# Norms and reciprocals spread over rows through DRAM instead of TensorE transposes, an earlier second load, and a changed order of shares and closings in a two-layer convolution-attention kernel

## The chip, the cores and the metric

The kernel runs on one core of one Trainium2 chip. The metric is the device time of one execution in microseconds (us). Three timed executions of the kernel before gave 1650.42, 1654.32 and 1650.83 us; the median is 1650.83 us. The operands of all products are stored as float32.

The engines are named as in the profile: PE is TensorE's matmul, PEld its weight load, DVE is VectorE, ACT is ScalarE, POOL is GpSimd, and SP is SyncE, which here only issues DMAs. An engine's name with a q behind it (SPq) is that engine's sequencer.

## The reference

The input x has 4 images of 32 channels by 128 x 128 pixels. Layer 0 folds each 2 x 2 block of pixels into channels: an image is then 128 channels of 64 x 64 = 4096 positions. The attention is between positions: the energy of two of them is the product of their 128 channels divided by the two positions' norms. Layer 1 takes the result as 4096 tokens of 128 values per image: a linear attention (all its products are sums over tokens, without a softmax), then a router and the two best of eight experts.

```python
xs = fold(x)                                   # 2x2 pixels into channels
q = xs.reshape(B, C * R * R, hw)
energy = einsum('bci,bcj->bij', q, q)          # 4096 x 4096 for each image
d = sqrt(diagonal(energy))
energy = energy / (d[:, :, None] * d[:, None, :])
attn = softmax(energy, axis=-1)
out = einsum('bcj,bij->bci', q, attn)
x = unfold(gamma * out + xs)
t = tokens(x)                                  # 4096 tokens of 128 values per image
t = t + linear_attention(layer_norm(t), Wk, Wq, Wv)
t = t + top2_experts(layer_norm(t), router_w, router_b, expert_w, expert_b)
```

The energy matrix of an image is 4096 x 4096 and symmetric. The kernel divides every position's channels by the position's norm before the product (`qn`). Two vectors per image have to be turned from "one value per partition" (a position on each partition) into "one value per column" (positions along the free dimension, the same on every partition): the reciprocal norms, which scale q, and the reciprocals of the softmax's sums times gamma, which scale the output.

## The kernel before, in words

**The attention of an image (`attend`).** The 4096 positions are cut into 8 chunks of 512. For each row i of chunks and each column jc up to i, four steps j each compute 128 x 512 energies (`pe`, line 609), which ACT turns into exponentials with their sums (`pr`, line 612); two steps later the values are multiplied in (`po`, line 497). Because the matrix is symmetric only the lower half is computed. The mirrored half comes from the same exponentials. DVE turns them in blocks of 32 x 32 (`F`, line 421), SP stores them in DRAM (`blocks<-F`, line 530) and reads them back with the blocks exchanged (`F<-blocks`, line 545), and PE then multiplies them in as a "transposed share" (`transposed_share`, `pg`, line 433), four matmul steps per tile, while ACT sums the same tile (`junk`, line 438) and DVE adds the result into `o` (line 442).

**The order is written out by hand.** All instructions of PE, DVE, ACT and SP stand in the order in which the Python code issues them; POOL's own order is left to the scheduler but for pinned instructions. `attend` is a generator that yields twice per step. A virtual `clock` advances by the work issued: 8 for a full energy step and 4 for a share step. A share may start when the clock has moved on by `LAG` = 57 since its tile's reload was issued; `step_share` runs one share step if the oldest is due. `after(n, f)` runs f n steps later. Around this run side streams: entries of `timed` (steps of a generator spread between two percentages of an image's clock; every count is two steps of the generator), and `steady` closings, stepped about once per attention step.

**Preparation of a pair of chunks (`prep`, `prep_first`).** Four DMAs load the pair (`xa`), DVE turns it (`turn_quarters`), squares and sums it (`squares`), POOL takes the power of -1/2 (line 164). To spread the norms along rows, DVE copies them 64 wide (`wide`, line 388), PE transposes that in four pieces (`pnorm`, line 399), and DVE multiplies the pair's channel rows by the result (`scale`, line 372) to give `qn`, the operand of both sides of `pe`. The very first pair (`prep_first`) is instead scaled before it is transposed (`ptn`, line 344). There are 16 pairs of chunks: one goes through `prep_first`, 15 through `pnorm`.

**The closing of an image (`layer1`).** From 84% of an image's clock on, its closing runs beside the next image's attention. `close_rows(kc)` for kc = 0 to 3 waits until the chunks 2kc and 2kc+1 are complete, takes the reciprocals of the sums (`den`, `rd`), copies them 64 wide (`rdx`, line 749), has PE transpose them (`pbd`, line 771), multiplies `o` by them into `df` (line 758), adds that to the tokens `T`, and takes the layer norm's statistics (`bs_a`, `close_stats`: six small DVE instructions, then POOL's power). ACT then normalises four rows of tokens at a time (`normalise`, line 696), and PE adds up their products (`pgram`). `attention_rows(u)` for u = 0 to 3 applies the linear attention (`pat`), takes statistics again, computes the router's logits and normalises; after u = 1 and u = 3 `sorted_experts` sorts tokens by expert, scatters and gathers them with POOL's indirect DMAs (`place` holds their places), and stores the image. The last image has nothing beside it: what is left of its closing (`last_parts`) is the end of the kernel.

**SP's queue.** SP issues nearly all DMAs, in order. DMAs share eight completion semaphores in rotation, and a DMA is issued only when the one eight places before it on its semaphore has landed.

Of the kernel before, what the change touches and what calls it, by code (L numbers as in the profile page):

```python
# [22 lines left out]
def kernel(  # L23
# [278 lines left out]
    def load_quarters(b, kc, queues=(nc.sync, nc.sync)):  # L302

        xa = xin.tile([P, 2, 2, 2, HW2, 2], F32, tag="xx", name=f"xa_{b}_{kc}")
        halves = x[b].rearrange("c (s g) w -> c s (g w)", s=2)
        for a in (0, 2, 1, 3):
            first_row = 16 * kc + 4 * a
            queues[a // 2].dma_start(
                xa[ts(a, S)].rearrange("p s k r w e -> p s (k r w e)"),
                halves[:, :, first_row * W : (first_row + 4) * W],  # L310
            )
        return xa

    def turn_quarters(s, xa, qT):
        for k in range(2):
            nc.vector.transpose(
                qT[:, s, 2 * k : 2 * k + 2, :].rearrange("p h (e r c) -> p r (h e) c", e=2, r=2),
                xa[:, s, k].rearrange("p r (h t) e -> p (r h) e t", h=2),
            )

    def prep_first(st):

        b, kc = 0, 0
        st["T"] = big1.tile([P, KT, D], F32, tag="T", name="T_0")
        xa = load_quarters(b, kc, (nc.sync, nc.scalar))
        qT = chunks_of(b, kc, st)
        yield
        ss = stat.tile([P, 2 * NJ], F32, tag="ss", name=f"ss_{b}_{kc}")
        rn = stat.tile([P, 2 * NJ, 1], F32, tag="rn", name=f"rn_{b}_{kc}")
        for s in range(2):  # L330
            turn_quarters(s, xa, qT)
            squares(b, kc, s, qT, ss)
            pow_neg_half(rn[:, ts(s, NJ), 0], ss[:, ts(s, NJ)])
        keep_running(40, ps_g, "pg")
        scaled = []
        for s in range(2):
            qs = work.tile([P, NJ, P], F32, tag="qs", name=f"qs_{b}_{kc}_{s}", bufs=2)
            nc.vector.tensor_tensor(qs, qT[:, s], rn[:, ts(s, NJ)].to_broadcast([P, NJ, P]), ALU.mult)
            scaled.append(qs)
        for s, qs in enumerate(scaled):  # L340
            qn = channels(b, kc, s, st)
            pt, done = hold(f"ptn_{b}_{kc}_{s}", lambda p, qn=qn: nc.scalar.activation(qn, p, AF.Copy))  # L342
            for j in range(NJ):
                nc.tensor.transpose(pt[:, ts(j, P)], qs[:, j, :], ident)
            done()
            yield

    def prep(b, kc, st):
# [3 lines left out]
        ahead = 2 if b == 0 and kc == 1 else 5  # L352
        xa = load_quarters(b, kc)
# [3 lines left out]
        for _ in range(ahead):  # L357
            yield
        qT = chunks_of(b, kc, st)
        for s in range(2):  # L360
            turn_quarters(s, xa, qT)
            yield
# [15 lines left out]
        rn = stat.tile([P, 2 * NJ, 1], F32, tag="rn", name=f"rn_{b}_{kc}")  # L378
        for s in range(2):
            squares(b, kc, s, qT, ss)  # L380
            if s == 1:
                pow_neg_half(rn[:, :, 0], ss)
            yield
        for _ in range(ahead - 2):
            yield
        wide = work.tile([P, NJ, 2, 64], F32, tag="qs", name=f"wide_{b}_{kc}", bufs=2)
# [3 lines left out]
        if b:  # L390
            yield
# [21 lines left out]
    def after(ticks, f):  # L413
        queued.append((tick[0] + ticks, f))
# [59 lines left out]
    def attend(b, st):  # L474
# [11 lines left out]
        for i in range(NCH):  # L486
# [94 lines left out]
            for jc in order:  # L581
# [21 lines left out]
                for j in range(NJ):  # L603
# [10 lines left out]
                    own.append(pr)  # L614
                    if ending and jc == order[-1] and j == NJ - 1:
                        st["exps"] = True
                    after(2, partial(values, pr[:, c0:], t, c0, CH))
                    if jc < i and not both:
                        after(1, partial(nc.vector.transpose, Fb[:, :, :, j, :], pr))
                        if j == NJ - 1:  # L620
                            after(2, partial(move, F, i, jc))
                    elif jc == i and not ending:
                        if j < NJ - 1:
                            after(1, partial(turn_blocks, F, pr, j))
                        if j == NJ - 2:
                            after(2, partial(move_diagonal, F, i))
                    elif jc == i and j in (1, 2):

                        after(1 if j == 2 and order[-1] == i else 2, partial(below, own, (2, 1) if j == 1 else (3,)))
                    turn_tick()  # L630
                    clock[0] += 2 * (CH - c0) // P
                    step_share()
# [21 lines left out]
    def layer1(b, st):  # L654
# [9 lines left out]
        place = stat.tile([P, 2, KT], U32, tag="place", name=f"place_{b}")  # L664
# [63 lines left out]
        def close_rows(kc):  # L728
# [10 lines left out]
            while "exps" not in st if last_rows else missing():  # L739
                yield from idle(1)  # L740
            while b > 0 and kc == 0 and not states[b - 1].get("sorted"):
                yield from idle(1)
# [3 lines left out]
            wide = work.tile([P, NJ, 2, 64], F32, tag="grp", name=f"rdx_{b}_{kc}", bufs=2)  # L746
            for s in range(2):
                one = rd[:, ts(s, NJ)][:, :, None]
                nc.vector.tensor_scalar(wide[:, :, s], one.to_broadcast([P, NJ, 64]), gam, None, ALU.mult)
            df = work.tile([P, 8, HW2, 2], F32, tag="df", name=f"df_{b}_{kc}", bufs=1)  # L750

            def divide(pb):
                for s in range(2):
                    own = slice(s * 64, s * 64 + 64)
                    o = st["o"][2 * kc + s]
                    for r2 in range(2):
# [4 lines left out]
                            pb[own].rearrange("p (j a t) -> p a j t", a=4, t=S),  # L761
# [3 lines left out]
            yield  # L765
            if not last_rows:
                yield
                yield
            pb, done = hold(f"pbd_{b}_{kc}", divide)
            for j in range(NJ):  # L770
                nc.tensor.transpose(pb[:, ts(j, P)], wide[:, j].rearrange("p s c -> p (s c)"), ident)
            yield
            while missing():
                yield from idle(1)
            done()
# [4 lines left out]
            nc.vector.tensor_tensor(tk, tk, df.rearrange("p k w r -> p k (w r)"), ALU.add)  # L780
            bs, stats = batch_stats("a", 8 * kc, 8)
            for j in range(8):
                stats[j]()
                if j == 3:
                    yield
                    yield
            close_stats("a", 8 * kc, 8, bs)
# [155 lines left out]
        def attention_rows(u):  # L943
# [17 lines left out]
            for j in range(8):  # L961
                stats[j]()
                if j == 3:
                    yield
                    yield
            logits = router_rows(nc.vector, 8 * u, 8, la)
            close_stats("f", 8 * u, 8, bs)
            next(logits)
            yield
# [450 lines left out]
    next(first)  # L1420
    load_weights()
    next(first)
    next(second)
    load_tokens(states[0]["T"][:, 0:8, :], 0, 0, 8)

    ordered = ExitStack()
    ordered.enter_context(tc.manual_schedule(engines=ENGINES))
    timed = [(first, 0, 1, 2), (second, 0.5, 5.5, 10)]
    for b in range(B):
# [36 lines left out]
        if b + 1 < B:  # L1466
            timed.append((prep(b + 1, 2, nxt), 0.5, 16, 17))
            timed.append((prep(b + 1, 3, nxt), 38, 62, 17))
# [43 lines left out]
```

## Time and profile before

The profiled execution took 1650.83 us, of which the span from the first to the last instruction is 1649.0 us.

| | before |
|---|---|
| median of 3 runs | 1650.83 us |
| profiled execution, its span | 1650.83 us, 1649.0 us |
| PE busy | 1609.9 us, 98% of the span |
| DVE, ACT, POOL busy | 931.5, 898.5, 593.8 us |
| DMA moved | 345.37 MB, 212 GB/s over the span |
| granted TensorE clock, mean | 0.996 |

A group row of the profile names the line, the engine and the operation, what is written and read, the count, then the busy time, the mean length of one instruction in ns, and the idle time of the engine just before it with what ended that idle time. Matmuls overlap, so a row's mean length is more than the spacing of two of them. In a row of waits, the total is followed by the number of waits and the longest one. In the timeline, the first two numbers are start and length in us.

### The profile page before, as it was taken

The numbers are of one execution on the slowest core, as the hardware profiler recorded it, in microseconds if no ns is written. First come the engines' busy times: TensorE is split into PE (matmuls) and PEld (weight loads), VectorE is DVE, ScalarE is ACT, GpSimd is POOL, SyncE is SP. The second block draws the span as 40 slices with busy tenths as digits, with TensorE's granted clock in tenths as the row PEclk, the third lists the DMA queues.
The fourth block names the chain that finished last, engine by engine and source line by source line (L and its number), as shares of the span: only waits on it lengthen the run. The fifth ranks groups of instructions, "written<-read, shape, count | busy, mean of one in ns | idle before, by whom it ended". The sixth has DMA issues, their size and how long they took to land.

```text
span 1649.0 us, 21309 instructions
## 1 busy us (share of the span) xinstructions
PE 1609.9 (98%) x5192; PEld 846.5 (51%) x5192; DVE 931.5 (56%) x2383; ACT 898.5 (54%) x2839; POOL 593.8 (36%) x565
## 2 busy tenths in 40 slices
PE   8999999999999999999999999999999999999987
PEld 4444544455554455555554455555554455555633
DVE  4543353567586443549478443448658634345786
ACT  3555445466475555547556455556656555545386
POOL 1000000001015441446555543256555652437166
PEclk9999999999999999999999999999999999999999
DMA  4655656676759777997899777798699877886001
GB/s 143 205 179 178 197 187 213 222 231 204 168 196 283 239 222 220 266 257 200 211 221 287 253 236 241 222 268 230 196 209 279 275 248 236 248 251 192 14 14 39
DMA packets 304297, 345.37 MB, mean 209 GB/s; under 512 B 82096, under 2 KB 230704, under 8 KB 289840
## 3 DMA queue, kind: packets, MB, share of 16 engines
q1 hardware_dynamic: 269712, 304.50, 59.9%
q0 software_dynamic: 26624, 25.58, 7.6%
q10 hardware_dynamic: 7840, 13.93, 2.9%
q8 instruction: 44, 0.72, 0.2%
q14 instruction: 77, 0.63, 0.1%
HBM read 167.08 MB, written 182.09 MB: 212 GB/s over the span
## 4 chain that ended last, share of the span: by engine, by line
PE 81%; DVE 7%; DMA 5%; ACT 3%; SPq 2%; issue 1%; POOL 1%; ACTq 0%; DVEq 0%; POOLq 0%
PE po L497 24%; PE pe L609 23%; PE pg L433 20%; PE pys L1130 3%; PE py L1304 3%; PE pg L453 2%; PE pys L1137 2%; PE pgram L725 2%; DMA F<-blocks 1%; DVE F L421 1%; DMA blocks<-rows 1%; SPq L938 1%; ACT pr L612 1%; ACT xn L696 1%; DMA blocks<-F 1%
## 5 line engine op out<-in xcount | busy, mean ns | idle before, releaser
L612 ACT ACTIVATE pr<-pe 128x512 f32<-128x512 f32 (+1 forms) x576 | 322.4, 560 | 547.5 <-PE pe L609 507.0
L497 PE MATMUL po<-pr,qT 128*128 128x512 f32 (+3 forms) x1152 | 549.4, 559 | 4.2 <-ACT o L502 3.9
L609 PE MATMUL pe<-qn,qn 128*128 128x512 f32 x896 | 458.8, 594 | 4.6 <-ACT pr L612 4.6
L433 PE MATMUL pg<-F,qT 128*128 128x512 f32 x880 | 449.8, 593 | 4.7 <-DMA F<-blocks 4.7
L421 DVE STREAM_TRANSPOSE F<-pr 128x512 f32<-128x512 f32 x440 | 305.4, 700 | 134.5 <-ACT pr L612 124.7
L497 PEld LDWEIGHTS po<-pr,qT 128*128 128x128 f32 x1152 | 215.2, 190 | 250.2 <-issue 217.9
L1178 POOL DMA_INDIRECT acc<-ys,place x128 | 202.1, 1579 | 209.1 <-ACT pr L612 134.8
L438 ACT ACTIVATE junk<-F 128x512 bf16<-128x512 f32 x440 | 273.0, 620 | 4.9 <-DMA F<-blocks 4.9
L433 PEld LDWEIGHTS pg<-F,qT 128*128 128x128 f32 x880 | 166.8, 190 | 199.4 <-issue 182.3
L1066 POOL DMA_INDIRECT xs<-xn,place x192 | 186.0, 969 | 184.1 <-ACT pr L612 118.9
L609 PEld LDWEIGHTS pe<-qn,qn 128*128 128x128 f32 x896 | 155.6, 191 | 119.1 <-issue 106.7
L442 DVE TENSOR_TENSOR o<-o,pg 128x512 f32<-128x512 f32 x110 | 75.1, 683 | 205.4 <-PE pg L433 205.2
L1112 DVE TENSOR_TENSOR results<-pys,xn 128x256 f32<-128x256 f32 x120 | 49.9, 416 | 187.2 <-ACT xn L1106 168.5
L164 POOL TENSOR_TENSOR rn<-ss,neg_half 128x8 f32<-128x8 f32 (+1 forms) x17 | 27.2, 1602 | 320.0 <-DVE ss L296 319.9
L612 ACT ACTIVATION_READ_ACCUMULATOR pr<-pe 128x1 f32 x576 | 111.9, 194 | 0.0
L1106 ACT ACTIVATE xn<-pys 128x256 f32<-128x256 f32 x120 | 45.2, 377 | 111.4 <-PE pys L1137 111.4
L1130 PEld LDWEIGHTS pys<-ew_sb,xn 128*128 128x128 f32 x468 | 70.5, 191 | 52.2 <-issue 49.7
L609 PE MATMUL pe<-qn 128*128 128x512 f32 (+3 forms) x256 | 91.4, 440 | 0.7 <-ACT qn L342 0.7
L1178 POOL DMA_INDIRECT yb<-ys,place x64 | 60.8, 950 | 81.1 <-DMA F<-blocks 31.1
L438 ACT ACTIVATION_READ_ACCUMULATOR junk<-F 128x1 f32 x440 | 84.5, 192 | 0.0
L1130 PE MATMUL pys<-ew_sb,xn 128*128 x468 | 71.6, 275 | 0.0
L1304 PE MATMUL py<-ew_sb,xn 128*128 128x512 f32 x128 | 61.5, 622 | 5.1 <-ACT tmp L1260 3.9
(217 smaller groups left out, 1463.2 us busy)
## 6 DMA issues: line engine op xcount, KB each, us to landing
blocks<-F SPq DMA_DIRECT2D x110, 1024.0 KB
F<-blocks SPq DMA_DIRECT2D x220, 192.0 KB
F<-blocks SPq DMA_DIRECT2D x220, 128.0 KB
xn<-xs SPq DMA_DIRECT2D x114, 132.0 KB
ys<-results SPq DMA_DIRECT2D x114, 128.0 KB
F<-blocks SPq DMA_DIRECT2D x220, 64.0 KB
below<-F SPq DMA_DIRECT2D x31, 384.0 KB
T<-in_x_dram SPq DMA_DIRECT2D x64, 128.0 KB
```

Source lines behind the costliest of these rows:

```text
L421: f()
L433: nc.tensor.matmul(pg.rearrange("p (a f) -> p a f", a=4), st["qT"][i][:, ib, :], G[:, :, ib], start=(ib == 0), stop=(ib == NJ - 1),)
L438: nc.scalar.activation(junk, G[:, :, ib], AF.Copy, accum_out=st["sums"][:, NJ * i + ib, jc : jc + 1])
L442: nc.vector.tensor_tensor(st["o"][jc], st["o"][jc], pg, ALU.add)
L497: nc.tensor.matmul(row["po"][:, lo:hi], qT[blk // NJ][:, blk % NJ, :], w, start=start, stop=(row["left"] == 0))
L609: nc.tensor.matmul(pe[:, c0:], qn[jc][:, ts(j, P)], qn[i][:, c0:], start=True, stop=True)
L612: nc.scalar.activation(pr[:, c0:], pe[:, c0:], AF.Exp, accum_out=sums[:, t, i : i + 1]).ins
L1066: inst = nc.gpsimd.indirect_dma_start(xs[h], offset(place[:, i, k : k + 1]), xn[:, k, :], None)
L1112: nc.vector.tensor_tensor(result[:, :n], p[:, 2 * P : 2 * P + n * D].rearrange("p (j c) -> p j c", c=D), bufs[g % 6][:, :n, D : D + 1].to_ ...
L1130: nc.tensor.matmul(p[:, 2 * P + j * D : 2 * P + j * D + D], bufs[6 + g % 2][:, j, :D], weights[:, bass.ds(begins[2 * (g % 2) + j], D)], st ...
L1178: inst = nc.gpsimd.indirect_dma_start(to, None, ys, offset(place[:, i, k : k + 1]), compute_op=op)
L1304: nc.tensor.matmul(bank, xn[:, k, :D], ew_sb[:, 4 * h : 4 * h + 4, :], start=True, stop=True)
```

## The change

The change has seven parts.

1. A new generator `spread_over_rows` writes a 128 x 32 tile of norms with DVE's block transpose, stores it in DRAM (16 KB), and reads it back with two DMAs, each of which puts the same 4 x 128 values on 64 partitions (128 KB each). It takes the place of the 64-wide copy, the four PE transposes and their PSUM bank in 14 of the 15 calls of `prep` (all but the second pair of image 0), and in `close_rows` for kc < 3 (12 of the 16 calls). The norms sit in three constant tiles, set to 1.0 by POOL at the start.
2. `close_rows` for kc < 3 computes its reciprocals as soon as its sums are complete (`seen`), and not only when `o` is; new sets `divided` and `added` keep the order among the closings of an image.
3. The second pair of image 0 is loaded into a `work` buffer right behind the first, ahead of the weights' and the tokens' loads; its turns stand between the DVE instructions of `prep_first`; its later steps run from 1.3% of the clock instead of 0.5%.
4. `prep_first` turns and squares the second half while POOL takes the first half's power, and the 40 warming transposes are issued first.
5. In a row's first tile at step 2, a share step is taken before the values' matmul instead of after it, if one is due at that earlier clock.
6. `close_rows` has one more yield ahead of `close_stats` (except in the last image's late rows), and `attention_rows` three more around `close_stats` and the first half of the logits.
7. `place` has one buffer instead of two; the next image's fourth pair is prepared at 36 to 54% instead of 38 to 62%.

```diff
-    def load_quarters(b, kc, queues=(nc.sync, nc.sync)):
-        xa = xin.tile([P, 2, 2, 2, HW2, 2], F32, tag="xx", name=f"xa_{b}_{kc}")
+    def load_quarters(b, kc, queues=(nc.sync, nc.sync), place=(xin, "xx")):
+        xa = place[0].tile([P, 2, 2, 2, HW2, 2], F32, tag=place[1], name=f"xa_{b}_{kc}")
...
+    norms = [const.tile([P, S], F32, tag=f"norm{n}", name=f"norm_{n}") for n in range(3)]
+    for norm in norms:
+        nc.gpsimd.memset(norm, 1.0)
...
-        for s in range(2):
-            turn_quarters(s, xa, qT)
-            squares(b, kc, s, qT, ss)
-            pow_neg_half(rn[:, ts(s, NJ), 0], ss[:, ts(s, NJ)])
-        keep_running(40, ps_g, "pg")
...
+        keep_running(40, ps_g, "pg")
+        summed(0, rows_squared(0))
+        sq = rows_squared(1)
+        st["turns"].pop(0)()
+        scale_rows(0)
+        summed(1, sq)
+        st["turns"].pop(0)()
+        st["turns"].pop(0)()
+        scale_rows(1)
+        st["turns"].pop(0)()
...
+    def spread_over_rows(norm, nm, tag, spread, gap):
+        turned = stat.tile([P, S], F32, tag="turned", name=f"turned_{nm}")
+        nc.vector.transpose(turned, norm)
+        yield
+        kept = dram.tile([P, S], F32, tag="norms", name=f"norms_{nm}", bufs=3)
+        nc.sync.dma_start(kept, turned)
+        for _ in range(gap):
+            yield
+        wide = work.tile([P, CH], F32, tag=tag, name=f"spread_{nm}", bufs=2)
+        for s in range(2):
+            nc.sync.dma_start(
+                wide[ts(s, 64)].rearrange("p (a f) -> p a f", a=4),
+                kept.rearrange("(a q) t -> a (q t)", q=S)[:, ts(s, P)].partition_broadcast(64),
+            )
+        spread.append(wide)
+        for _ in range(gap):
+            yield
...
+        if not on_chip:
+            yield from idle(1)
+            yield
+            spread = []
+            yield from spread_over_rows(norm, f"{b}_{kc}", "qs", spread, 5)
+            for s in range(2):
+                scale(s, spread[0], lambda ap: ap.rearrange("p (a j t) -> p a j t", a=4, t=S))
+            yield
+            return
...
+                    starts = jc == order[0] and j == 2
+                    if starts:
+                        step_share()
                     turn_tick()
                     clock[0] += 2 * (CH - c0) // P
-                    step_share()
+                    if not starts:
+                        step_share()
...
-        place = stat.tile([P, 2, KT], U32, tag="place", name=f"place_{b}")
+        place = stat.tile([P, 2, KT], U32, tag="place", name=f"place_{b}", bufs=1)
...
+            far = kc < 3
+            while not summed() if far else "exps" not in st if last_rows else missing():
                 yield from idle(1)
             den, rd = (stat.tile([P, 2 * NJ], F32, tag=nm, name=f"{nm}_{b}_{kc}") for nm in ("den", "rd"))
             nc.vector.tensor_reduce(den, st["sums"][:, ts(kc, 2 * NJ), :], AX.X, ALU.add)
             nc.vector.reciprocal(rd, den)
+            if far:
+                norm = norms[2]
+                nc.vector.tensor_scalar(norm[:, : 2 * NJ], rd, gam, None, ALU.mult)
+                spread = []
+                yield from spread_over_rows(norm, f"den_{b}_{kc}", "grp", spread, 5)
...
             while missing():
                 yield from idle(1)
-            done()
+            if far:
+                divide(spread[0])
+            else:
+                done()
+            st["divided"].add(kc)
...
+            if not late_rows:
+                yield
             close_stats("a", 8 * kc, 8, bs)
...
+            yield
             logits = router_rows(nc.vector, 8 * u, 8, la)
             close_stats("f", 8 * u, 8, bs)
+            yield
             next(logits)
             yield
+            yield
             nc.sync.dma_start(t2[:, ts(u, 8)], T[:, ts(u, 8), :])
...
-    next(first)
-    load_weights()
-    next(first)
-    next(second)
+    next(first)
+    next(second)
+    load_weights()
+    ordered.enter_context(tc.manual_schedule(engines=ENGINES))
+    next(second)
+    next(first)
     load_tokens(states[0]["T"][:, 0:8, :], 0, 0, 8)
...
-    timed = [(first, 0, 1, 2), (second, 0.5, 5.5, 10)]
+    timed = [(first, 0, 1, 2), (second, 1.3, 5.5, 8)]
...
-            timed.append((prep(b + 1, 3, nxt), 38, 62, 17))
+            timed.append((prep(b + 1, 3, nxt), 36, 54, 17))
```

## The prediction

> **What bounds the kernel now.** First the page's busy times and its chain.
>
> ```profile
> PE 1609.9 (98%) x5192; PEld 846.5 (51%) x5192; DVE 931.5 (56%) x2383; ACT 898.5 (54%) x2839; POOL 593.8 (36%) x565
> ...
> PE 81%; DVE 7%; DMA 5%; ACT 3%; SPq 2%; issue 1%; POOL 1%; ACTq 0%; DVEq 0%; POOLq 0%
> ```
>
> PE is in use for 98% of the span and is 81% of the chain. So a PE instruction taken out counts in full, and other engines count only where PE waits. Next, PE's waits and the one large wait of SP's queue:
>
> ```profile
> PE pg L433 <- DMA F<-blocks: 4.7, 3, 1.9
> PE pe L609 <- ACT pr L612: 4.6, 3, 1.6
> ...
> PE po L497 <- ACT o L502: 3.9, 16, 0.5
> PE pnorm L399 <- DVE wide L388: 2.6, 2, 2.4
> PE ptn L344 <- DVE qs L338: 2.6, 1, 2.6
> ...
> SPq L545 <- DMA blocks<-F: 248.5, 70, 6.6
> ```
>
> All PE waits together are some 31 us. The 4.6 is three equal places; the timeline of one shows their origin:
>
> ```profile
> 871.79 1.68 POOL L164 TENSOR_TENSOR rsf<-dm_f,neg_half 128x8 f32<-128x8 f32 x1 [1.44 <-DVE sv_f L688]
> ...
> 873.84 0.27 POOL L692 TENSOR_SCALAR nbo<-nbf 128x8 f32<-128x8 f32 x1
> ...
> 874.14 1.65 ACT L696 ACTIVATE xn<-T,nbo,rsf 128x128 f32<-128x128 f32 x4 [3.80 <-POOL nbo L692]
> ...
> 876.41 1.13 PE L609 MATMUL pe<-qn,qn 128*128 128x512 f32 x2 [1.56 <-ACT pr L612]
> ```
>
> ACT's in-order queue stood 3.80 us at a normalise that waits for POOL's power; `pr` behind it came late, and PE lost 1.56. Then start and tail:
>
> ```profile
> 21.95 0.49 DVE L388 COPY wide<-rn 128x256 f32<-128x256 f32 x2 [1.13 <-POOL rn L164]
> ...
> 22.50 0.66 PE L399 MATMUL pnorm<-ident,wide 128*128 128x128 f32 x4 [2.39 <-DVE wide L388]
> ```
>
> ```profile
> 1529.02 0.60 PE L771 MATMUL pbd<-ident,rdx 128*128 128x128 f32 x4
> ...
> 1529.45 1.02 PE L609 MATMUL pe<-qn,qn 128*128 128x512 f32 x2
> ...
> 1549.44 4.86 PE L186 MATMUL spare<-ident 128*128 128x128 f32 x36
> ...
> 1551.46 1.65 ACT L696 ACTIVATE xn<-T,nba,rsa 128x128 f32<-128x128 f32 x4 [3.84 <-POOL nba L690]
> ...
> 1554.13 1.95 PE L725 MATMUL pgram<-xn 128*128 128x128 f32 x16
> ```
>
> From 1539.7 on PE waits for the last closings: `spare` transposes fill 4.86 us while DVE, POOL and ACT finish the rows.
>
> **What the Trainium skill says.** "TensorE: Matmul & The Clock Gate", Part 4: PE-mode transpose, gives about 275 ns to a 128 x 128 transpose inside a kernel. The trace's windows agree (`pbd` 273, `pnorm` 275), but they overlap: from 1529.02 to 1529.45 four take 0.43 us, 0.109 each. I price groups so. Part 1: The HAM clock gate, halves the clock after an idle window of 3.4 us; the trace grants half speed from 11.59 to 15.0 us. "DMA: Bandwidth & Descriptors", Two DMAs through the same engine are not ordered: a DMA that reads what another wrote must be held by its issuing engine until the first has landed. The trace agrees: SP's 248.5 us above are reloads held for the stores of their blocks. The same page's Latency and other measured facts puts a DMA's fixed cost near 2 us; this trace's landings after the issue have medians from 2.5 (`out`) to 4.9 us (`blocks<-F`, 1 MB); its 16 KB store is not in it.
>
> **The change part by part**, against the profiled execution (1650.83, which is also the median, so nothing is converted).
>
> *Groups removed.* 14 `pnorm` and 12 `pbd` groups go: 26 x 0.43 = 11.2 us of PE, in stretches where PE is in use. **-11.2.** Their DVE copies go too: 28 of 30 `wide` x 0.27 = 7.5 us, 24 of 32 `rdx` x 0.37 = 8.9; 26 small transposes and 12 multiplies (about 0.2 each, as L745's) come in. DVE is 56% busy: nothing either way.
>
> *What the spread adds.* 78 DMAs on SP: per spread a store (about 0.4 us of issue, as `t<-T` 0.42 and `blocks<-F` 0.37) and two reloads (0.5 each): 26 x 1.4 = 36 us in SP's queue, against an end of issuing attention near 1530. The reloads wait for the store, and behind them in SP's queue stand F stores, F reloads, tokens. Store issue to landing is bounded by 2 and 5 us, and five yields stand between: by the order of the changed program's instructions, laid over the times of before, 4 to 10 us, so it has usually landed when SP gets there. From the reloads to DVE's `scale` stand 3.9 to 10 us in the same way, to `divide` 4 to 30. Issue (1.0), landing (3.3, the median of `F<-blocks` of like size) and SP's own lag (1 to 3 us) need 5 to 7, so the shortest, five spreads of the norms at 3.9 to 6.4, may stall DVE by 0 to 3 us. Behind it stand `F` transposes and `o` adds; `pr` has six buffers, so PE notices only about four steps, 10 us, later, and I take nothing for that (if the buffers are full by then, 5 x 1.5 = 7.5 at most). F reloads land 8 us ahead of their `pg` on average, 5.5 where spreads will stand, 1.9 in the tightest places. Those tight places are where I charge: a gain is excluded, since nothing gets earlier on SP; at most every fourth of 26 spreads pushes a reload late by its 1.4 us, 26 / 4 x 1.4 = 9. I take the lower part, as only three `pg` waits exist now: **+2.5** (0 to 9).
>
> *Start.* The `ptn` wait: reordering DVE so that the first scaling is not behind both squarings, with the clock's warming first, brings `qs` from 9.74 to 9.25 to 9.95: -0.5 (0 to -1). The second pair's loads were issued at 7.67 and stood for a buffer; now they are issued behind the first's from about 2.1, held by the semaphores' rotation to some 6, landing near 8.3; its first turn is wanted at 8.9. So its power ends near 17 instead of 21.91, and the 2.39 us wait goes: -2.4 (to 0 if the loads come after 13). Weights and tokens move behind these four DMAs (2.5 us of SP); they are wanted later. **-2.9.** POOL's three memsets (about 0.15 each) delay `ident` and the warming by 0.5 us at most; data come only at 5.62.
>
> *Closings drawn apart.* One to three more yields lie between `close_stats` and `normalise`: one attention step, 2.6 us, which outweighs the 1.56 at each of three places. **-4.6** (-2.5 to -4.6). What ACT waits for is POOL's power and two short POOL instructions, from 871.79 to 874.11; no indirect DMA of POOL's is moved ahead of them on purpose, but POOL's order is a scheduler's, and one such DMA (1.6 us) in front would eat most of the step: hence the weaker end. The other closings get later by half a step to a step, hidden by attention.
>
> *Share first.* `po` waits for ACT's `o` at 16 row starts: about 0.25 each. The share is due at the earlier clock only in rows 1 and 2 of images 1 to 3; elsewhere the step has none there, and rows that had one after lose it. By the order of instructions that is a gain in some rows and a loss in others: **-0.6** (-2 to +0.5). A `pnorm` wait of 0.26 at 382 goes: **-0.3**.
>
> *Tail.* In the last image the rows of chunk 1 divide right behind their last `o` add, their sums having come from memory before; the token adds and two `gram` sums (0.67 and 0.68) that now stand between the steps of the last closing (at 1541.19 and 1547.07) come ahead of it. The last `df`, at 1542.09, starts 0.8 earlier; with 1.35 for the two sums and some 0.85 for rows that need not be turned any more there, the last `pgram` at 1554.13 starts 3 us sooner: **-3.0** (-1 to -4; +2 if the spread of rows 2 lands late, since its reload is queued on SP behind a put of results that waits for gathers). `place` with one buffer: its writer waits for gathers of the image before, which now stand some 20 us earlier in the program: nothing, else 3 us of DVE. Fourth pair at 36 to 54%: PE's work is the same: nothing.
>
> The sum: -11.2 - 2.9 - 4.6 - 0.6 - 0.3 - 3.0 + 2.5 = -20.1, so 1630.7; I say **1630.5**.
>
> **Rivals.** *Only the groups pay (0.20).* The waits of ACT move to another closing and the tail's chain (DVE 2.79, 1.23, POOL 1.63, ACT) stays: -11.2 - 2.9 + 4 = 1640.7, 1636 to 1643. For it: three of the six normalise waits of the same kind cost PE nothing now and may do so at their new places. Against: the yields are a whole step. *More is gained (0.04)*: SP's charge is nil and the tail takes -5: 1618 to 1624. *SP as the bound (0.06), slower.* A spread's reload holds SP's in-order queue until its store has landed, and the F reloads behind it are late for `pg`. The gains are 22.6, so it decides from 22.6 / 26 = 0.87 us of PE wait per spread. A hold of 8 us against a mean reserve of 6.8 gives 1.2 x 26 = +31: 1659. For it: 248.5 us of such holds and reserves of 1.9. Against: the five yields, and PE waited for reloads three times in 110. *No net change (0.02)*: the same at 0.87. That the change does not do what it says holds for the share-first part, counted above. The forecast itself has 0.68.
>
> **How the numbers follow.** 0.3% (5 us) is what a measurement can tell. The forecast's own range is 1625 to 1637, from the ends of the terms that can go together: SP's 0 to 9 and the tail's 1 to 4. To leave no more than 2 in 10 outside I add rival one up to 1643 and half of the better one: 1622 to 1644. Faster: 0.68 + 0.20 + 0.04 = 0.92; same 0.02; slower 0.06.
>
> **What would show it.** PE busy down by some 11; `pnorm` at 4 and `pbd` at 16 transposes; no `pe` wait of 1.5 from ACT; no `pnorm` wait over 1; the last `pgram` 3 us closer to its attention's end. Wrong if the wait of `pg` for F reloads rises above 10 us, if DVE's rows `scale` and `df` show waits for the reloads that reach `pr`, or if the second pair's loads land after 13 us.

## The result, and the profile after

The changed kernel takes 1667.6 us (median of 4) against 1650.6 us for the kernel before: the ratio is 1.0096, with a 95% interval of 1.0075 to 1.0117. It is 17 us slower, where 20 us faster was forecast. The profiled execution took 1664.5 us with a span of 1662.7 us, so the two traces differ by 13.7 us of span.

The page after, busy times and chain:

```profile
PE 1614.5 (97%) x5088; PEld 840.6 (51%) x5088; DVE 920.5 (55%) x2369; ACT 900.7 (54%) x2839; POOL 593.3 (36%) x568
...
PE 83%; DMA 7%; DVE 3%; ACT 2%; SPq 2%; issue 1%; POOL 0%; ACTq 0%; DVEq 0%; POOLq 0%
```

PE has 104 instructions fewer, which are the 26 groups of four, and is nevertheless busy for 4.6 us longer. Part of its time was at a lower clock. PE's waits after (total, times, longest):

```profile
PE pg L511 <- DVE o L500: 8.5, 2, 4.3
PE pgram L789 <- ACT xn L760: 8.0, 5, 5.0
PE pys L1225 <- DMA xn<-xs: 5.6, 5, 2.7
PE pg L491 <- DMA F<-blocks: 4.1, 2, 2.1
PE po L555 <- ACT o L560: 3.4, 17, 0.5
```

The waits that were to go are gone: no `pe` behind ACT's normalise, no `pnorm` behind `wide`, `ptn` down from 2.6 to 1.2. The first row is new; the second and third were 0.6 and 0.7 us before. What DVE waited for shows why:

```profile
DVE qT L315 <- DMA xa<-in_x_dram: 28.5, 4, 9.3
DVE df L835 <- DMA ys<-results: 10.4, 2, 5.3
DVE qn L422 <- DMA spread<-norms: 9.1, 3, 4.4
...
DVE turned L374 <- DMA norms_den<-turned_den: 4.2, 1, 4.2
```

In the kernel before DVE waited once for `xa`, at the start (5.6 us). The timeline at the beginning of image 2 shows the worst of it (one stretch of SP, ACT and DVE, then of PE and ACT):

```profile
750.70 8.66 SPq L308 DMA_DIRECT2D xa<-in_x_dram  x4
...
755.94 0.33 ACTq L1254 DMA_DIRECT2D acc<-t  x1
...
761.56 1.45 DVE L315 STREAM_TRANSPOSE qT<-xa 128x256 f32<-128x256 f32 x4 [9.34 <-DMA xa<-in_x_dram]
...
776.82 1.65 PE L511 MATMUL pg<-F,qT 128*128 128x384 f32 x2 [4.27 <-DVE o L500]
...
778.27 0.49 ACT L760 ACTIVATE xn<-T,nba,rsa 128x128 f32<-128x128 f32 x1 [6.34 <-POOL nba L754]
```

Four loads whose issuing takes 2.5 us otherwise took SP 8.66 us. The first three went out by 752.8 us, the fourth at 758.80. It has the same completion semaphore (number 104 in the trace) as the `acc<-t` before it in the rotation of eight. In this trace the DMAs that SP and ACT issue carry the eight numbers 100 to 107, and those of POOL have eight of their own, 111 to 118: the rotation is shared by SP and ACT alone. That `acc<-t` is issued by ACT, which came to it only at 755.94; it landed at 758.78, and SP went on 0.02 us later. DVE stood 9.34 us for `xa`, everything behind it was late, and 15 us later PE stood 4.27 us. Image 3 has the same at 1150 to 1172 us.

A stall of this length has a second price. The windows of the trace around it (length, PE busy, granted clock, DMA share, GB/s):

```profile
765.00:771.00 6.00, 6.00 (x20) 1.00 0.77 207
771.90:775.00 3.10, 0.65 (x3) 1.00 0.77 253
776.80:782.00 5.20, 4.83 (x12) 0.50 0.80 172
783.00:790.00 7.00, 7.00 (x29) 1.00 0.78 183
```

After the stall PE works at half speed for up to 6.83 us. Over the whole program, leaving out the last microseconds, half speed was granted for 34.1 us after and for 10.2 us before.

The tail, for the lines shown of before, has become shorter:

```profile
1562.62 4.13 PE L186 MATMUL spare<-ident 128*128 128x128 f32 x36
...
1568.26 1.65 ACT L760 ACTIVATE xn<-T,nba,rsa 128x128 f32<-128x128 f32 x4 [5.71 <-POOL nba L754]
```

From the last `po` to the last 16 products of `pgram` (1568.81) it is 11.0 us, before 16.5 us.

The books balance. I take for every form of PE instruction the 30th percentile of the distance from its start to the next one's as its norm. All that PE spends beyond that sums to 53.5 us before and 79.1 us after. The norms of the removed work are 11.3 us. So 25.6 - 11.3 = 14.3 us are lost, and the spans say 13.7. By stretches, the first 50 us go from 9.4 to 5.9, and most of the loss lies around the changes to images 2 and 3: 700 to 800 us goes from 0.9 to 12.1, 1050 to 1200 from 1.4 to 14.6.

### The profile page after: what moved, and what is told of

It is laid out like the page before. It is cut to its first block, busy times and chain, and to the rows that moved or that the text cites. A ratio compares the mean times of both kernels' runs of the same rounds, so it can differ in the third digit from the quotient of the medians.

```text
span 1662.7 us, 21158 instructions
## 1 busy us (share of the span) xinstructions
PE 1614.5 (97%) x5088; PEld 840.6 (51%) x5088; DVE 920.5 (55%) x2369; ACT 900.7 (54%) x2839; POOL 593.3 (36%) x568
## 4 chain that ended last, share of the span: by engine, by line
PE 83%; DMA 7%; DVE 3%; ACT 2%; SPq 2%; issue 1%; POOL 0%; ACTq 0%; DVEq 0%; POOLq 0%
PE po L555 25%; PE pe L667 23%; PE pg L491 20%; PE pys L1218 3%; PE py L1392 3%; PE pg L511 2%; PE pgram L789 2%; PE pys L1225 2%; DMA F<-blocks 1%; PE pat L940 1%; SPq L603 1%; DMA xn<-xs 1%; DMA blocks<-F 1%; ACT xn L760 1%; ACT tmp L1348 1%
## 5 line engine op out<-in xcount | busy, mean ns | idle before, releaser
L164 POOL TENSOR_TENSOR norm<-ss,neg_half 128x8 f32<-128x8 f32 (+1 forms) x17 | 27.0, 1590 | 359.9 <-DVE ss L296 352.4
L164 POOL TENSOR_TENSOR rsa<-dm_a,neg_half 128x8 f32<-128x8 f32 x16 | 27.7, 1731 | 118.3 <-DVE sv_a L752 118.3
```

The source lines that it names most:

```text
L164: pinned(nc.gpsimd.tensor_tensor(dst, src, neg_half.to_broadcast(list(src.shape)), ALU.pow))
```

## The experiments

The variants ran on five chips. On four of them the kernel before has medians from 1659.4 to 1662.4 us, on the fifth (`b_best_share` and `a_best_noshare`) 1650.8 us. Every ratio is to the kernel before on the same chip, with its 95% interval; on one of the four the changed kernel itself was repeated (`after_again`). Theory 1 is that a DMA of ACT's queue holds SP through the shared rotation. Theory 2, nearest to the slower rival of the prediction, is that the spreads' own traffic and their reloads' waits for stores hold SP.

### The reloads of ACT off the rotation

```diff
-                nc.scalar.dma_start(accs[g], t2[:, ts(g, 4)])
+                nc.gpsimd.dma_start(accs[g], t2[:, ts(g, 4)])
```

> The changed kernel (1667.6 us), but the 32 reloads acc<-t are issued from POOL's queue instead of ACT's, so that they leave the rotation of eight completion semaphores that SP's DMAs share. Theory 1 (the loss comes from the rotation: acc<-t, issued late by ACT, holds the SP DMA eight places behind it, and in the changed order that is a load of xa which DVE needs at once): DVE's two waits of 9.3 us for xa fall below 5, PE's two waits of 4.2 us at 776 and 1172 go with their 6.8 us of half clock, 14 to 18 us less, 1650 to 1655 us. Theory 2 (the loss is the spreads' own traffic on SP, 78 DMAs and reloads held for stores): at most 6 us less, 1661 to 1668 us, and the waits for xa stay over 5 us. If POOL stands in front of the normalise powers, ACT's waits for nba grow and some of the gain is lost.

Measured: 1644.2 us, ratio 0.9897 (0.9879 to 0.9916). DVE's waits for `xa` are at most 4.2 us after the start, PE's stalls at 776 and 1172 are gone, and SP is held by ACT's DMAs for 57 us instead of 141 (stops of over 1 us; what is left is image 0's loads). The gain is larger than I expected, some 30 us by the ratios. PE's time beyond the norm is 58.7 us, against 88.6 in the repeat of the changed kernel; 22 of these 30 us lie in the two stretches around the changes of image. One stall more went with it: in the changed kernel ACT itself stood 8.20 us at 1524.93, where its own queue held an `acc<-t` that waited for its buffer's last store, and PE lost 5.0 us there. So this edit removes two things, the rotation and ACT's wait for the buffer; the second is that one place. No run takes `acc<-t` out of the rotation and leaves it on ACT's queue.

The same edit in the kernel before:

> The kernel before with only its 32 reloads acc<-t moved from ACT's to POOL's queue. SP is held by acc<-t for some 90 us in it too, but for DMAs with a reserve. Theory 1: little is gained, ratio 0.996 to 1.001 (PE's waits for F at 851 and 1240, 1.8 us each, may go). If it gains as much as the changed kernel did from the same edit (1.2% to 2%), moving acc<-t is a gain by itself and the comparison with it says nothing on what the change lost.

Measured: 1654.8 us, ratio 0.9955 (0.9941 to 0.9968). A little gain, not the 2% that the changed kernel had from it.

### Without the spreads

`on_chip = True` for every pair puts the 14 groups of `prep` back, with the yields that the kernel before has around them; `far = False` puts the 12 of the closings back, and gives up the earlier reciprocals of part 2 with them.

```diff
-            far = kc < 3
+            far = False
```

> The changed kernel with the reciprocals of the closings transposed by PE again (12 groups of four, +5.2 us of PE), the norms of prep still spread through DRAM. Theory 2: the twelve spreads of the closings cost about half of the 25 us of new waits, so 1667.6 - 12 + 5 = 1660 us, and PE's wait for F at 338 goes. Theory 1: the place of acc<-t against SP's DMAs is a matter of the order of the closings, which this changes too; waits for xa of 9 us either stay (1668 to 1673 us) or go with the order and not with the traffic (1650 to 1657 us), while SP's total time held by acc<-t stays near 80 us.

Measured: 1669.8 us, ratio 1.0064 (1.0041 to 1.0087), with DVE still waiting 9.4 and 9.5 us for `xa`.

```diff
-        on_chip = b == 0 and kc == 1
+        on_chip = True
```

> The changed kernel with the norms of prep transposed by PE again (14 groups, +6.1 us of PE), the closings' reciprocals still spread. Theory 2: the fourteen spreads of prep cost about half of the new waits; 1667.6 - 12 + 6 = 1661 us, with DVE's waits for spread norms (4.4, 2.6, 2.1 us) gone. Theory 1: the two 9.3 us waits for xa and PE's 4.2 us stay, as the closings and their acc<-t stand where they stood: 1668 to 1674 us.

Measured: 1677.0 us, ratio 1.0096 (1.0073 to 1.0120); waits for `xa` of 9.3 and 9.2 us.

> The changed kernel with no spread at all: only the start, the shares, the drawn apart closings, place and the fourth pair's times are left (26 groups back, +11.3 us of PE). Theory 2: all new waits go, 1650.6 - 3.5 (start) - 5 (ACT's three waits) - 3 (tail) = 1637 to 1643 us, faster than before. Theory 1: the loss is not the spreads', so it stays above 1650 us unless the order happens to part acc<-t from xa.

Measured: 1677.0 us, ratio 1.0094 (1.0075 to 1.0113); waits for `xa` of 9.5 and 9.4 us. Theory 2 falls as the main cause: without a single spread the changed order is as slow. The spreads aren't free in it, though. With all the groups back PE has 11.3 us more work, and its time beyond the norm is 80.2 us, against 88.6 in the repeat of the changed kernel: most of what the spreads save here is lost again in waits. One place shows it: at 337.70 us PE waited 2.14 us for an `F` whose reload stood in SP's queue behind that of a spread, which SP held until 329.75 for a store issued at 324.90.

### Without the added yields

> The changed kernel with part 6 undone (no yields added to the closings). Theory 1a (the drawn apart closings moved acc<-t by some steps against the next image's load of xa, to exactly eight DMAs ahead of it): DVE's two waits of 9.3 us for xa and PE's two stalls of 4.2 us go, ACT's three waits of 3.8 us with PE's 1.5 us may come back, ratio to before 0.993 to 1.001. Against it (the meeting of acc<-t and xa comes from other parts): the waits for xa stay at 9 us and the ratio at 1.007 to 1.013.

Measured: 1719.6 us, ratio 1.034 (1.030 to 1.038). This is far off both expectations. The closings, not drawn apart, ask ACT for `xn` while POOL's powers are late behind a DVE that waits for DMAs. PE's first row of waits there is:

```profile
PE pgram L789 <- ACT xn L760: 26.5, 10, 8.9
```

So the yields protect the kernel with spreads. ACT's three waits of 3.8 us came back too, but PE lost only 0.51 to 0.55 us at each, not 1.5.

> The changed kernel with neither spreads nor the added yields: left are the earlier start, the shares, the earlier reciprocals' order, place and the fourth pair's times. Theory 1a: as without the yields nothing meets, the start's 3.5 us are gained and little else moves: ratio 0.995 to 1.001, waits for xa under 5 us. Against it: as with the yields, ratio 1.006 to 1.012 with waits for xa of 9 us.

Measured: 1677.9 us, ratio 1.0093 (1.0061 to 1.0125), DVE waiting 6.8 and 7.0 us for `xa`. Theory 1a, that the yields brought `acc<-t` in front of `xa`, is wrong. Without spreads the yields make no difference to the time (1.0094 with them, `a_both_te`).

### The share's place

In the trace of this last kernel, without spreads and yields, each of ACT's 24 `acc<-t` has 4 to 9 exponentials fewer ahead of it than in the kernel before. With part 5 alone all 24 stand behind exactly as many as there, so their place is part 5's doing. Part 5 alone in the kernel before:

```diff
+                    starts = jc == order[0] and j == 2
+                    if starts:
+                        step_share()
                     turn_tick()
                     clock[0] += 2 * (CH - c0) // P
-                    step_share()
+                    if not starts:
+                        step_share()
```

> The kernel before with part 5 alone (the share ahead of the values in a row's first tile). In the order of instructions that brings acc<-t 4 to 8 steps forward (from the 298th exponential to the 293rd for the fifth of image 0), with no spread, no added yield and no other change. Theory 1b: SP is then held by acc<-t just ahead of the load of xa, DVE waits 6 to 9 us for it at the start of images 2 and 3, PE stalls there and the clock halves: ratio 1.005 to 1.015. If part 5 is harmless by itself (the loss needs the thinner reserves that the other parts make), the ratio is 0.998 to 1.003.

Measured: 1679.3 us, ratio 1.0096 (1.0070 to 1.0121). These few lines alone cost more than the whole change: 16.9 us, against 11.8 us in the repeat of the changed kernel on the same chip. The timeline of this kernel (SP, ACT and DVE, then PE):

```profile
754.90 0.33 ACTq L1170 DMA_DIRECT2D acc<-t  x1
757.62 0.34 SPq L554 DMA_DIRECT2D below<-F  x1
758.00 2.49 SPq L308 DMA_DIRECT2D xa<-in_x_dram  x4
...
762.79 1.42 DVE L316 STREAM_TRANSPOSE qT<-xa 128x256 f32<-128x256 f32 x4 [6.63 <-DMA xa<-in_x_dram]
...
784.19 0.66 PE L775 MATMUL pbd<-ident,rdx 128*128 128x128 f32 x4 [2.80 <-DVE rdx L753]
```

SP issued nothing for 12.05 us before 757.62. The DMA it wanted to issue was eight behind `acc<-t`, which landed at 757.55; its own data had been ready since 742.69. The loads of `xa` stood behind it. PE's time beyond the norm grows from 0.9 to 9.1 us between 700 and 800 us and from 1.4 to 6.9 between 1050 and 1200.

Undone in the changed kernel:

> The changed kernel with part 5 undone (no share ahead of the values in a row's first tile). In the order of instructions that moves acc<-t later against attention: the fifth one of image 0 stands behind the 302nd exponential instead of the 295th, and the load of xa that it held stands near the 294th. Theory 1b (the share's place sets the clock at which the closings are stepped, so part 5 brought the closings 4 steps forward and acc<-t to eight places ahead of xa): DVE's 9.3 us waits for xa go below 5 us, PE's 4.2 us stalls with 6.8 us of half clock go, ratio to before 0.992 to 1.002. Against it: ratio 1.006 to 1.012 with the waits for xa at 9 us.

Measured: 1677.6 us, ratio 1.0101 (1.0068 to 1.0135). The mechanism moved as expected, the time did not: the changed kernel is as slow without part 5. The 9.3 us waits for `xa` are gone, and others took their place (DVE's waits for DMAs in this kernel):

```profile
DVE qn L422 <- DMA spread<-norms: 18.4, 5, 6.6
...
DVE df L835 <- DMA ys<-results: 14.1, 2, 7.3
DVE qT L315 <- DMA xa<-in_x_dram: 8.1, 2, 6.0
```

### The load of `xa` wanted later

```diff
-        ahead = 2 if soon else 5
+        ahead = 2 if soon else 9
```

> The changed kernel with four more yields between the load of xa and its first turn (nine instead of five), nothing else: SP is held by acc<-t as before, but DVE asks for xa some 7 us later. Theory 1 (the two 9.3 us waits of DVE for xa are worth 14 to 16 us: PE's 4.2 us twice and 6.8 us of half clock twice): ratio 0.999 to 1.003, against 1.0096 for the changed kernel, with PE's stalls at 776 and 1172 gone. If the waits are only the place where SP's lateness shows first, the stalls come back at the next thing DVE needs (spreads, df) as they did without part 5: ratio 1.006 to 1.012.

Measured: 1671.1 us, ratio 1.0050 (1.0032 to 1.0067). The changed kernel as it is, on the same chip:

> The changed kernel as it is, beside the other runs on their chip: the ratio 1.0096 (1.0075 to 1.0117) again, with the same waits for xa, so that the runs of the variants can be set against it and not only against the kernel before.

Measured: 1674.2 us, ratio 1.0078 (1.0053 to 1.0104). DVE no longer waits for `xa` after the start, and only 3 us are gained. PE now waits for `F` instead:

```profile
PE pg L491 <- DMA F<-blocks: 11.1, 4, 3.2
```

So the late `xa` was the first sign of a late SP, not the whole loss. SP is held for 140 us by ACT's DMAs in this kernel as well.

### Nothing but SP in the rotation

First, besides `acc<-t`, the weights' loads and the filling of `xs` went to POOL's queue, with their places left to the scheduler:

> The changed kernel with acc<-t and also the reloads that ACT issues in image 0 (weights, and the filling of xs) on POOL's queue, so that nothing but SP is left in the rotation. Theory 1: SP's holds of 14, 12, 6, 6 and 5 us in image 0 go, and with them PE's waits for F at 181 and 338 (2.2 and 3.3 us and 3.4 us of half clock each): 5 to 8 us under the version with acc<-t alone, ratio 0.984 to 0.988. Theory 2: the wait at 338 stays, as there SP stood for the store of a spread; ratio 0.987 to 0.990.

Measured: 1639.2 us, ratio 0.9862 (0.9831 to 0.9893). The fillings ran ahead, to 15 us and later, and PE has a stall of 4.6 us at 41. Pinned to their places in the order, where that stall is gone:

```diff
-            inst = nc.scalar.dma_start(xs[g // 8][ts(g % 8, step), :], rows[ts(g, step), :])
+            inst = pinned(nc.gpsimd.dma_start(xs[g // 8][ts(g % 8, step), :], rows[ts(g, step), :]))
```

> The changed kernel with nothing but SP in the rotation, and the fillings of xs and the weights' loads kept in their places on POOL's queue (in the run before they ran ahead to 18 us and crowded image 0's first tiles: a stall of 4.6 us at 41). Theory 1: that stall and its half clock go, 4 to 7 us under the 0.986 of that run: ratio 0.981 to 0.985.

Measured: 1631.4 us, ratio 0.9801 (0.9771 to 0.9831), the fastest version of all. PE's waits:

```profile
PE py L1392 <- ACT tmp L1348: 4.0, 4, 2.4
PE pe L667 <- ACT pr L670: 4.0, 1, 4.0
PE po L555 <- ACT o L560: 2.9, 14, 0.5
PE ptn L367 <- DVE qs L349: 2.4, 1, 2.4
PE pgram L789 <- ACT xn L760: 2.1, 1, 2.1
```

No wait for `F` is left, and none for `xn<-xs`. From landing to use, reloads of `F` now have 10.7 us in the mean and never under 3; in the changed kernel it is 8.6 with 13 of 110 under 3, in the kernel before 7.9 with 11. The same moves in the kernel before:

> The kernel before with the same moves to POOL's queue. The change's own worth without the rotation is the ratio of the changed kernel's version to this one: the forecast of the whole (20 us of 1651) says 0.988. Ratio of this run to before: 0.993 to 0.997 (acc<-t alone gave 0.9955; PE's wait for F at 184 goes too).

Measured: 1649.5 us, ratio 0.9915 (0.9888 to 0.9942). So without the rotation the change is worth 1631.4 / 1649.5 = 0.989, or 18.1 us. Its waits show what the change removes (three of the four `pe` behind ACT, and `pnorm` behind `wide`):

```profile
PE pe L609 <- ACT pr L612: 6.7, 4, 2.1
...
PE pnorm L399 <- DVE wide L388: 2.7, 2, 2.5
```

The version of 1631.4 us with all 26 groups back and no spread (the "run before" is that version):

> As the run before, but with all 26 groups transposed by PE again and no spread. It measures what the spreads are worth when nothing is coupled. The forecast's term: 26 groups x 0.43 = 11.2 us, less its charge of 2.5 for the spreads' traffic (0 to 9): 2 to 11 us slower than the run before, ratio 0.983 to 0.992. Theory 2 (the spreads' traffic eats their gain): not slower than the run before.

Measured: 1657.0 us, ratio 0.9961 (0.9943 to 0.9978). The spreads, with the earlier reciprocals of part 2, are worth 25.7 us here, more than both theories had. By the norms 11.3 us are the groups; the rest is PE's time beyond the norm, 60.4 against 48.7 us: the tail from the last `po` is 16.1 us long instead of 11.0, and `pbd` waits 1.2 us for `rdx` at three places. This kernel is also 7.5 us slower than the kernel before with the same moves (1649.5 us): without the spreads the rest of the change is a loss even here.

> The kernel before with ACT's reloads on POOL's queue, and part 5 alone. Part 5 alone cost the kernel before 1.0% (1.0096). If that loss is the place of acc<-t in the rotation, part 5 costs nothing here: the ratio of the version without it, 0.9915 (0.989 to 0.994), within 0.3% either way. If the share's place or the earlier closings are slow by themselves, the ratio is 0.998 or more.

Measured: 1646.2 us, ratio 0.9971 (0.9963 to 0.9978), against 1.0096 for part 5 with the rotation. The expected ratio was missed. It ran on the chip where the kernel before takes 1650.8 us, and the version without part 5 was not run there, so the ratio isn't to be set beside 0.9915. PE's time beyond the norm can be: 50.8 us here and 52.9 without part 5, 4 of which are a stop that only the other chips have (see the end). PE waits more for `o` (7.2 us instead of 3.2) and for `rdx` (3.4 instead of 0), and less at `pe` (1.7 instead of 6.7, 2.1 of which are the stop). So part 5 by itself costs some 2 us by this count, not 16.9.

> The fastest version (the changed kernel with nothing but SP in the rotation, 0.980) with part 5 undone. The forecast gives part 5 a gain of 0.6 us (2 us to a loss of 0.5): ratio 0.979 to 0.982. If part 5 carries part of the 18 us that the change gains there, for instance by its earlier closings, the ratio is above 0.984.

Measured: 1634.1 us, ratio 0.9900 (0.9869 to 0.9932), on that chip too, where the version with part 5 was not run. PE's time beyond the norm is 47.9 us against 48.7 with part 5, of which 7 us are a stop near 1303 that only the other chips have (see the end). So part 5 is worth some 6 us at most here, and the ratio alone can't say; the forecast's 0.6 us is neither confirmed nor refuted.

> The fastest version so far (only SP in the rotation, ratio 0.980) with two more yields between xa and its turn: there DVE still waits 2.3 and 3.2 us for xa, which PE does not feel. Expected the same within 0.3%: 0.977 to 0.983. If it gained over 0.5%, those waits reach PE through something the waits do not show.

Measured: 1640.7 us, ratio 0.9864 (0.9837 to 0.9890), slower than without the two yields, where I expected no difference. PE stands 2.0 us at `pgram` at 765 and at 1151, each time with 3.4 us of half clock. Perhaps a later preparation meets a closing there; this was not followed.

## Why the prediction was wrong

**Groups removed (-11.2): right.** 104 transposes are gone and the norms of PE's work fall by 11.3 us.

**Start (-2.9): right.** The first 50 us beyond the norm fall by 3.5 us (by 2.0 between the two versions without the rotation).

**Closings drawn apart (-4.6): the waits are gone, but the yields earn only a third of it.** Part 5 alone, without a yield, already shortens each of PE's three waits from some 1.5 us to 0.52 to 0.56, and in the two kernels without the yields they are no longer than that. What the yields prevent instead, in the kernel with spreads, is the 26.5 us at `pgram`, which the prediction didn't have.

**Tail (-3.0): right in kind, too small.** The stretch from the last `po` fell by 5.5 us, part of which is `pgram` work that now runs earlier. It goes with the closings' spreads and earlier reciprocals: without them it is 16.1 us again (`a_best_te`).

**What the spread adds (+2.5, 0 to 9): within its range only without the rotation.** With only SP in the rotation no wait for `F` appears, and the reserve of the reloads falls by 1.5 us (12.1 without spreads, 10.7 with them). In the coupled kernel the spreads cost some 8 us, the difference of 80.2 and 88.6; one part of it is the wait at 338. DVE's stalls for late spreads were put at 0 to 3 us; three came, of 4.4, 2.6 and 2.1 us.

**Share first (-0.6, -2 to +0.5): this step failed.** I priced it by PE's waits for `o` alone, and asked only where the share becomes due. I didn't follow what else reads the clock that the share moves: the closings are stepped by it. A term of -0.6 us cost 16.9 us when it was made alone. In the order of instructions part 5 brings `acc<-t` of image 0's second half from the 298th exponential to the 293rd in the kernel before. That the pattern of clock steps does it follows from the code; why it is just these four to nine exponentials was not traced. The step is enough for the loss and not needed for it: without part 5 the changed kernel is as slow.

**The rotation was described and not priced: this step failed too, with part 5 and without it.** The sum has no term for the time that SP is held by ACT's DMAs; taking `acc<-t` away from ACT made the changed kernel some 30 us faster. Before the result the kernel's eight semaphores were written down, and SP's waits of before name `acc<-t` in four rows, which I passed over for the 248.5 us of stores. SP was held by ACT's DMAs for 133 us in the kernel before and for 141 after, in stops of over 1 us. The amount is nearly the same. What changed is what stood behind: a reload of `F` with 8 us in reserve before, the `xa` that DVE needed at once after. My slower rival had the right queue and the wrong holder. It asked for 0.87 us at each of 26 spreads; what came was seven stalls of 2 to 5 us. Of the signs of being wrong that the prediction named, PE's wait for the reloads of `F` stayed at 4.1 us, and the second pair was there by 9.3 us: they watched the spreads and the start, not ACT's DMAs.

**The half clock was cited and not priced.** The Trainium skill ("TensorE: Matmul & The Clock Gate", Part 1: The HAM clock gate) tells of a throttle after an idle window of about 3.4 us; I used it for the start alone. In these traces stalls from 2 us on were enough in most cases (counts at the end). 24 us more at half speed are about 12 us of PE's work by an estimate (half of 24), nearly as much as the stalls themselves.

Where the coupling is absent, 18 us are measured against 20 forecast, but that the sum is so near is in part luck. The spreads with what goes with them (groups, traffic and tail) bring 25.7 us there, where the forecast had 11.7; the rest costs 7.5 us, where the forecast had a gain of 8.4. Runs show that part 5 alone brings such a loss to the kernel before, and that the loss goes when ACT's DMAs leave SP's rotation, in the changed kernel and in the kernel with part 5 alone. Still open is how the loss in the changed kernel without part 5 divides between its parts: there the spreads, the results' stores and `xa` are late in turn.

## What to carry to other kernels

When DMAs of two queues share completion semaphores, each of them can be a hidden wait in the other queue; list for every DMA of the slower queue the one that comes eight later, and ask how soon that is needed. Move such DMAs to a queue of their own before judging any change of order, or every edit is measured with its luck in the rotation. A virtual clock that paces side streams is an interface: an edit that shifts it by one step must be followed through all that reads it.

## What the runs showed of the hardware that I had not expected

How long PE may stand before the clock halves shows in the stalls of 1.5 us and more between 30 and 1540 us, counted over all twenty profiles. Of 20 between 1.5 and 1.9 us one was followed by half speed (1.65 us at 887.8 in `a_best_noshare`), of 50 between 1.97 and 2.95 us 32 were, and all 29 of 3.18 us or more were. Half speed came in steps of 3.41 us, two or three of them after 16 of the 23 longest stalls (3.9 us and more). By an estimate, half of 3.41, a stall just over 2 us can so cost up to 1.7 us more.

A DMA of ACT that SP needs for nothing stopped SP for 12.05 us (the line at 757.62 above), through the semaphore only: the data that SP's own DMA needed were ready 2.9 us before the stop began.

In the changed kernel the 16 KB stores of the norms landed 3.3 us after the end of their issue in the median and those of the reciprocals 2.8, the 128 KB reloads 3.6 and 3.7: the small store is nearly as slow as a reload eight times its size.

On the four chips where the kernel before takes 1659 to 1662 us, PE stands for 2 to 6 us near 1300 to 1380 us in nearly every profile, mostly behind an exponential of ACT. In the profiles from chips where it takes 1651 us it doesn't. The cause is open. Kernels compared on those four chips both have it, and the two kernels from the fifth, `b_best_share` and `a_best_noshare`, are therefore not set beside them by their times.
